# Routing tokens by indirect transfers instead of matmuls, a softmax from two exps, and a clamp on another engine, in a two-layer graph and state-space kernel

## The chip, the cores and the metric

The kernel runs on one core of a Trainium2 chip. The metric is the device time of one execution in microseconds; lower is better. Engines are named as the profile names them: PE is TensorE, DVE is VectorE, ACT is ScalarE, POOL is GpSimd, and SP is SyncE, which here only issues transfers. Each engine works through its own instructions in a fixed order, and an instruction that has to wait holds up all that stand behind it on that engine.

## What is computed

The input x holds 64 batches of 256 tokens with 256 features. Two layers follow each other; each is a graph attention part and then a feed-forward part, both added to x. `adj` is a random 256x256 adjacency matrix.

```python
# layer 0
x = x + gnn0(layernorm(x))    # MLP to 512, attention over all tokens, MLP to 256, attention masked by adj
x = x + ffn0(layernorm(x))    # only the top tokens go through the MLP
# layer 1
x = x + gnn1(layernorm(x))    # attention masked by adj
x = x + ffn1(layernorm(x))    # a Mamba-2 block: convolution, decays, chunk of 256

# each attention:
e = leaky_relu(f1[:, :, None] + f2[:, None, :], 0.2)   # f1, f2: one number per token
att = softmax(where(mask, e, -inf), axis=2)
out = elu(att @ h)

# ffn0:
weights = x @ wr + br                       # one number per token
sel_idx = top_k(weights, 128)[1][:, :127]   # the 127 best of 256 tokens
y = (gelu(x[sel_idx] @ w1 + b1) @ w2 + b2) * weights[sel_idx]
out = zeros.at[sel_idx].set(y) + x
```

In the Mamba block a matrix E of decays is needed for every head: the exp of the difference of two running sums, clamped so that the part that a triangular mask drops later does not overflow.

## The kernel before

A step works on a group of two batches, 512 tokens, that is four chunks of 128 tokens on the 128 partitions. There are 32 groups; the first and the last are worked on as two single batches. Everything is float32. A matmul of float32 stands in the trace as two passes, a transpose as one.

Each part of a layer is a Python generator that issues a few instructions and then yields. A lane is a sequence of such parts over the groups: lane a is `gnn0`, lane b is `ffn0` and then `gnn1`, lane c is `ffn1`; lanes d, e and f are the single batches at the two ends, and w prepares the weights. Strings written out by hand, `FIRST`, `ORDER` and `LAST` (lines 21 to 37), say which lane takes the next step: `FIRST` at the start, then `ORDER` again and again (one pass for one group), then `LAST`. So three groups are in work at a time, in different parts of the layers, and each engine's order is fixed when the program is built.

The places that the change touches, with the line numbers of the profile:

- `scores` (L422 to L474), the attention weights, three times per group. PE transposes the column f2 into a row `fb` (L430). DVE finds the largest (L437, or L446 with the mask), computes `top` for each of the four chunks (L439 or L450) and from it `nm`, minus the row's maximum (L455). ACT applies Prelu (the leaky relu, L459) and then Exp with the row's sum as a by-product (L463). DVE takes the reciprocal (L468) and POOL scales (L473). `turned` (L489) transposes the result on PE.
- `ffn0` (L597 to L705). After the layernorm, DVE computes each token's weight `wc` (L602, L605); PE spreads it as a row `wrow` (L610). DVE counts for each token how many have a larger weight, which is its rank (L622, L625), and compares the rank with 0 to 126 (`ranks`, L120 to L125) to form the 0-1 matrix `pick` (L628). PE multiplies by `pick` to gather the 127 tokens, already transposed (`psel`, L635), transposes `pick` (L645, copied as `pT`, L647), runs the MLP (`ph`, `py`), and multiplies by `pT` to send the results back to their tokens (`po`, L695). DVE combines (L702), POOL adds to x (L705).
- In `ffn1`, the row of running sums goes to DRAM (`csd`, L786 and L787) and comes back spread over all partitions as E, one 384 KB load per head (L809). `decays` (L814 to L826) clamps the two diagonal blocks of E with one DVE instruction (L820) and takes the exp on ACT (L826). Later DVE multiplies E by `cb` (L899) and PE uses it (`py`, L916).
- All matmuls are issued by a helper at L251 and all transposes by one at L254, so PE's rows are told apart by their tiles.

Of the kernel before, what the change touches and what calls it, by code (L numbers as in the profile page):

```python
# [9 lines left out]
I32 = mybir.dt.int32  # L10
BF16 = mybir.dt.bfloat16
# [10 lines left out]
    "dwddadadwaaadawdaaddadaddaaaaadddaaddaaaaddaddaddadaaadaddaddwawdaaaaaaadddadddawdaaaaadadaadaddbaba"  # L22
    "aaabaaaabbaawaaaabwaabaaaaababbbaabbbwababababbbbabaaaabaabaawabababbaaaaabbbaaabbbbabbbaababbababab"
    "baababbbaaaabbabbbabbbaaacwccaababcaababbaabcaaabaaabacabbabbbbbaaabaabaabcbcabaabwbbaacabbaabawabca"
    "bbbab"
)
ORDER = (
    "cAaaccbbbbbbacabaccccbccaabacccabcbccabaacbccacabcaaaacacacbcccccbcacabcccbcaaacacbbccccccacaaccbcac"
    "cbacacabccabcccbcbBabccaccbcccabbcacaacbaccacbcbaacbcbbcbcababcbbcbCccbbbbaacaacabcaabbcbbabbbbbccc"
)  # L30
LAST = (
    "ececefefceecbbceccbbcbffbbbccfcbbfceccebbfcccbefccbcbeceebfcccecccecccceccfbccbcecccbccbeeccbefceccf"
    "ccccccfeeebbccecccfecffffcccfbffebcccbfbceffbccbcccefebbcefcccfceeebcbccccbfefccbcccbfbffcbbccccbcbb"
    "cfceefcbfbbcfefcbbcffbfecccbfcbfefbbbfbfbccffeeeebffbeccccfffebbfebbefbecfcbccccccbcbbcbffcccbeeceec"
    "ebfecbbbbcebffcceccbccccbeccebccececbbefcccffecfccffccfecfebcebceeceecebcffbcfeccfffcfecfeccefcececc"
    "cfe"
# [4 lines left out]
def kernel(ctx: ExitStack, tc: tile.TileContext, a: dict, out: bass.AP):  # L41
# [78 lines left out]
    ranks = cons("ranks", P, P)  # L120
    with tc.tile_pool(name="first", bufs=1) as first:
        iota_i = first.tile([P, P], I32, tag="iota_i", name="iota_i")
        nc.gpsimd.iota(iota_i, pattern=[[1, P]], base=0, channel_multiplier=0)
        nc.vector.tensor_copy(ranks, iota_i)
    nc.vector.memset(ranks[:, KK:P], -1.0)  # L125
# [75 lines left out]
    for t, ap in ((dtb, a["L1_ffn_dt_bias"]), (negA, a["L1_ffn_A_log"])):  # L201
# [28 lines left out]
        "xn": 2, "pk": 3, "v": 2, "g": 4,  # L230
# [6 lines left out]
    def tiled(pool, shape, tag, name, bufs):  # L237
        return pool.tile(list(shape), F32, tag=tag, name=name, bufs=bufs)
# [4 lines left out]
    def sm(tag, *shape, bufs=4):  # L243
        return tiled(small, shape, tag, tag, bufs)

    def sized_sm(tag, n, most, *rest, bufs=4):

        return sm(tag, P, most, *rest, bufs=bufs)[:, :n]
# [39 lines left out]
    def made_ready():  # L288
# [19 lines left out]
        nc.vector.tensor_scalar(mask1, adj, 0.0, -1e37, ALU.is_le, ALU.mult)  # L308
# [31 lines left out]
        yield  # L340
        for t in (b1h, conv_w, conv_b, W_in[:, :, :DI]):
            nc.vector.tensor_scalar(t, t, 0.5, None, ALU.mult)
# [23 lines left out]
    def sized(G, own=None):  # L366
# [12 lines left out]
        def columns(tag, name, most=512):  # L379
            t = wide(lambda tag, name: t512(tag, name) if most == 512 else tiled(t2, (P, most), tag, name, 4), tag, name)  # L380
            return t[:, (own or 0) * N : (own or 0) * N + T]
# [40 lines left out]
        def scores(f1, f2, mask, strict, tag):  # L422
# [3 lines left out]

            yield
            fb = psum("fb")
            for c in range(C):
                tr(fb[:, tok(c)], f2(c).to_broadcast([P, P]), ident)  # L430
            halves = [slice(h * N, (h + 1) * N) for h in range(2)]
            es = [t512(tag, "e") for b in range(G)]
            rows = [fb[:, b * N : (b + 1) * N] for b in range(G)]
            top = sized_sm("top", C, 4)
            if mask is None:
                most = sized_sm("most", G, 2)
                nc.vector.tensor_reduce(most, fb[:, :T].rearrange("p (b j) -> p b j", b=G), AX.X, ALU.max)  # L437
                for c in range(C):
                    nc.vector.tensor_scalar(  # L439
                        top[:, c : c + 1], most[:, c // 2 : c // 2 + 1], f1(c), -1.0, ALU.add, ALU.mult  # L440
                    )
            else:
                most = sized_sm("topm", C, 4)
                for c in range(C):
                    e = es[c // 2][:, halves[c % 2]]
                    nc.vector.tensor_tensor_reduce(  # L446
                        e, rows[c // 2], mask[:, c % 2, :], 1.0, -3e38, ALU.add, ALU.max, most[:, c : c + 1]
                    )
                for c in range(C):
                    nc.vector.tensor_scalar(  # L450
                        top[:, c : c + 1], most[:, c : c + 1], f1(c), -1.0, ALU.add, ALU.mult
                    )
            yield
            nm = sized_sm("nm", C, 4)
            nc.vector.scalar_tensor_tensor(nm, top, ALPHA, top, ALU.mult, ALU.min)  # L455
            den = sized_sm("den", C, 4)
            for c in range(C):
                e = es[c // 2][:, halves[c % 2]]
                nc.scalar.activation(e, rows[c // 2] if mask is None else e, AF.Prelu, bias=f1(c), alpha=ALPHA)  # L459
            yield  # L460
            for c in range(C):
                e = es[c // 2][:, halves[c % 2]]
                nc.scalar.activation(e, e, AF.Exp, bias=nm[:, c : c + 1], accum_out=den[:, c : c + 1])  # L463
            yield
            if strict:

                nc.vector.scalar_tensor_tensor(den, nm, 1e30, den, ALU.is_lt, ALU.mult)
            nc.vector.reciprocal(den, den)  # L468
            if strict:
                nc.vector.scalar_tensor_tensor(den, nm, 1e30, den, ALU.is_lt, ALU.mult)  # L470
# [33 lines left out]
        def project(xT, w, tag):  # L504

            res = []
            for c in range(C):
# [4 lines left out]
                h = tiled(t2, (P, D + 2), tag, "hp", 4)  # L512
                nc.scalar.copy(h, pp[:, : D + 2])
# [3 lines left out]
        def aggregate(at, h, i):  # L517

            u = psum("u")
            for half in range(2):  # L520
                for j in range(2):
# [3 lines left out]
                        h[2 * i + j][:, :D],  # L525
# [4 lines left out]
        def gnn0(xt, of, early):  # L530
            xn = yield from layernorm(xt, *of, "o")
            xT = yield from transposed(xn, lambda: columns("h", "xT", H1 + 2))
# [9 lines left out]
            h1 = []  # L542
# [539 lines left out]
```

## Time and profile before

| what | us |
|---|---|
| median of 3 runs (lowest, highest) | 3656.5 (3651.49, 3656.68) |
| the profiled execution's own time | 3653.81 |
| its span | 3652.1 |
| PE busy | 3533.4 |
| DVE busy | 2842.1 |
| ACT busy | 2189.1 |
| POOL busy | 1146.8 |
| TensorE clock granted | 0.99 |
| DMA: 150.89 MB, mean 41 GB/s; the SP queue's packets took 12.1% of the 16 engines' span | |

Busy time is the time in which an engine executed something; waits are not in it. An engine's rows add up to less or more than its share where instructions overlap, as matmuls do. A row of the groups gives the line, the engine, what is written and read, the shape and the count, then the busy time and the mean of one in ns, then the idle time of the engine just before these instructions and what ended it. The chain that ended last is followed back from the last instruction; 81% of it lies on PE.

### The profile page before, as it was taken

Reading aid. Unit: us, or ns where it says so; the run is one execution under the profiler, and the core shown is the slowest. Engines: PE = TensorE matmul, PEld = TensorE weight load, DVE = VectorE, ACT = ScalarE, POOL = GpSimd, SP = SyncE. Lnnn points to the kernel's source line nnn. Section 1 sums busy time; section 2 is a strip of 40 time slices with the busy share of each in tenths; the row PEclk is TensorE's granted clock in tenths of the full one; section 3 lists DMA queues with packets and bytes.
Section 4 is the critical chain, followed back from the end, with each engine's and each line's share of the span. In section 5 each row is a group of like instructions: output and inputs, shape, how many; then the busy total and the mean of one; then the engine's idle time right before and its main releaser. Section 6 shows DMA issues by size and latency. Waiting matters only on the chain.

```text
span 3652.1 us, 50662 instructions
## 1 busy us (share of the span) xinstructions
PE 3533.4 (97%) x17004; PEld 2550.6 (70%) x17004; DVE 2842.1 (78%) x7275; ACT 2189.1 (60%) x4942; POOL 1146.8 (31%) x1274
## 2 busy tenths in 40 slices
PE   8999999999999999999999999999999999999876
PEld 6766776776776776776776776776776777776544
DVE  5577778777778777878777878777878777878776
ACT  4565665665665665666665666655666655666544
POOL 2223333323333323333323333323333323333222
PEclk9999999999999999999999999999999999999989
DMA  3011101111101111101111101111101111101111
GB/s 116 1 39 43 49 15 43 48 42 46 49 15 43 48 40 48 49 15 43 48 40 49 48 16 43 49 40 49 44 20 43 48 40 49 41 23 37 43 43 48
DMA packets 90260, 150.89 MB, mean 41 GB/s; under 512 B 12304, under 2 KB 57232, under 8 KB 90000
## 3 DMA queue, kind: packets, MB, share of 16 engines
q1 hardware_dynamic: 90000, 147.65, 12.1%
q8 instruction: 135, 2.21, 0.2%
q14 instruction: 125, 1.02, 0.1%
HBM read 125.86 MB, written 17.56 MB: 39 GB/s over the span
## 4 chain that ended last, share of the span: by engine, by line
PE 81%; DVE 12%; ACT 4%; issue 1%; POOL 1%; DMA 1%; SPq 0%; ACTq 0%; POOLq 0%; DVEq 0%
PE pp L251 31%; PE u L251 10%; PE py L251 9%; PE po L251 7%; PE pz L251 6%; PE pt L254 5%; PE ph L251 4%; PE pa L251 3%; PE psel L251 2%; DVE st L393 1%; DVE xt L595 1%; DVE g L674 1%; DVE w L498 1%; DVE g L671 1%; DVE w L594 1%; PE pss L251 1%
## 5 line engine op out<-in xcount | busy, mean ns | idle before, releaser
L251 PE MATMUL pp<-W_fc,o 128*128 128x256 f32 (+1 forms) x2048 | 460.1, 379 | 0.4 <-DVE W_fc L286 0.4
L845 DVE SCALAR_TENSOR_TENSOR xs<-pp,conv_w,xs 128x510 f32<-128x510 f32 (+5 forms) x495 | 359.9, 728 | 93.9 <-ACT xs L841 79.9
L251 PEld LDWEIGHTS pp<-W_fc,o 128*128 128x128 f32 x2048 | 381.9, 189 | 67.8 <-issue 15.9
L826 ACT ACTIVATE E<-E,ncs 128x256 f32<-128x256 f32 (+1 forms) x1024 | 382.0, 449 | 61.0 <-DVE E L820 58.3
L473 POOL TENSOR_SCALAR e<-e,den 128x256 f32<-128x256 f32 x384 | 186.8, 505 | 714.2 <-PE pp L251 350.3
L251 PE MATMUL pp<-xT,W_in 128*128 128x512 f32 (+1 forms) x660 | 303.6, 593 | 0.0
L850 ACT ACTIVATE th<-xs 128x512 f32<-128x512 f32 (+1 forms) x165 | 101.7, 617 | 326.6 <-DVE xs L845 311.4
L925 POOL TENSOR_TENSOR xs<-xs,gz 128x512 f32<-128x512 f32 (+1 forms) x132 | 205.9, 1561 | 203.0 <-DVE xs L924 200.5
L251 PE MATMUL py<-w,g 128*128 128x256 f32 x1024 | 236.2, 383 | 20.7 <-DVE g L674 20.7
L899 DVE TENSOR_TENSOR E<-E,cb 128x768 f32<-128x768 f32 (+1 forms) x264 | 250.5, 964 | 1.1
L705 POOL TENSOR_TENSOR xt<-xn,xt 128x512 f32<-128x512 f32 x64 | 81.3, 1270 | 526.1 <-DVE xn L702 525.9
L251 PE MATMUL pz<-xT,W_in 128*128 128x512 f32 (+1 forms) x528 | 242.8, 583 | 0.0
L567 POOL TENSOR_TENSOR o<-w,o 128x512 f32<-128x512 f32 (+1 forms) x132 | 180.7, 1369 | 197.8 <-DVE w L501 197.8
L251 PE MATMUL ph<-sel,w 128*128 128x256 f32 x1024 | 242.0, 379 | 0.0
L251 PE MATMUL po<-W_ol,xs 128*128 128x256 f32 x1024 | 241.3, 379 | 0.0
L251 PEld LDWEIGHTS py<-w,g 128*128 128x128 f32 x1024 | 190.0, 190 | 70.9 <-DVE g L674 46.7
L251 PE MATMUL pp<-xT,mlp_w 128*128 128x512 f32 (+1 forms) x528 | 236.5, 583 | 0.7 <-ACT xT L419 0.7
L251 PE MATMUL u<-at,h 128*128 128x256 f32 x1024 | 236.8, 379 | 0.0
L251 PE MATMUL pp<-o,mlp_w 128*128 128x512 f32 (+1 forms) x528 | 231.1, 590 | 2.9 <-POOL o L567 2.9
L820 DVE TENSOR_TENSOR E<-E,ccs 128x512 f32<-128x512 f32 (+1 forms) x264 | 224.3, 863 | 0.0
L393 DVE BATCH_NORM_STATS2 st<-xt 128x6 f32<-128x256 f32 x512 | 185.1, 413 | 49.7 <-POOL xt L750 23.4
L251 PEld LDWEIGHTS u<-at,h 128*128 128x128 f32 x1024 | 191.7, 190 | 37.6 <-issue 7.3
(179 smaller groups left out, 7722.3 us busy)
## 6 DMA issues: line engine op xcount, KB each, us to landing
E<-csd SPq DMA_DIRECT2D x248, 384.0 KB
xt<-in_x_dram SPq DMA_DIRECT2D x31, 512.0 KB
out_dram<-xt SPq DMA_DIRECT2D x31, 512.0 KB
cs<-xs SPq DMA_DIRECT2D x64, 64.0 KB
E<-csd SPq DMA_DIRECT2D x16, 192.0 KB
w<-in_L_ffn_w_dram SPq DMA_DIRECT2D x2, 1024.0 KB
W_in<-in_L_ffn_W_in_dram SPq DMA_DIRECT2D x1, 1160.0 KB
mlp_w<-in_L_gnn_mlp_w_dram SPq DMA_DIRECT2D x2, 512.0 KB
```

Of the source, the lines that this page charges most:

```text
L251: nc.tensor.matmul(to, lhsT, rhs, start=start, stop=stop)
L254: nc.tensor.transpose(to, of, eye)
L393: nc.vector.bn_stats(st[:, c, :], xt[:, c, :])
L473: nc.gpsimd.tensor_scalar(e, e, den[:, c : c + 1], 1.0, ALU.mult, ALU.mult)
L567: nc.gpsimd.tensor_tensor(o1[m], w, o1[m], ALU.add)
L705: nc.gpsimd.tensor_tensor(pair(xt, b), xn[b], pair(xt, b), ALU.add)
L820: nc.vector.tensor_tensor(diag, diag, ccs[:, :, :, h : h + 1].to_broadcast([P, G, 2, P]), ALU.min)
L826: nc.scalar.activation(e[:, b, to], e[:, b, to], AF.Exp, bias=ncs[:, b, half, h : h + 1])
L845: nc.vector.scalar_tensor_tensor(s3[:, :, d:], p3[:, :, : N - d], conv_w[:, m, 3 - d : 4 - d], s3[:, :, d:], ALU.mult, ALU.add)
L850: nc.scalar.activation(th, s, AF.Tanh)
L899: nc.vector.tensor_tensor(e2, e2, cb2, ALU.mult)
L925: nc.gpsimd.tensor_tensor(yt, yt, gz, ALU.mult)
```

## The change

Four things are changed, and the three strings that fix the order are written anew for them.

1. **Indirect transfers.** A new lane g (`ranked_tokens`) runs ahead of lane b. It computes the ranks as before, but the row of weights goes to DRAM and comes back spread over the partitions (`wrow` is now in SBUF). POOL issues four indirect transfers per group that write each token's normalised features to the row of its rank in a DRAM tile; the first 128 rows are read back (`taken`), and four transposes on PE make `psel` of them. After the MLP the results go to DRAM (`ranked`), and four more indirect transfers read for every token the row of its rank, or of rank 127 at most, where `valid` and the changed b2 put zeros. `pick`, `pT`, and the two multiplications by them are gone.
2. **Softmax.** Instead of Prelu and then Exp, ACT takes two Exps of the row, with scale 1 and with scale 0.2, and DVE takes the larger of the two and sums it. The columns f1 and f2 are copied to a tile of their own.
3. **Clamp of E.** Four POOL instructions of 128x128 per head take the place of one DVE instruction of 128x512.
4. **Buffers.** `xn` has four buffers in place of two, a tag `row` is added, small tiles have three buffers in place of four.

```diff
@@ scores
-            nm = sized_sm("nm", C, 4)
-            nc.vector.scalar_tensor_tensor(nm, top, ALPHA, top, ALU.mult, ALU.min)
...
-                nc.scalar.activation(e, rows[c // 2] if mask is None else e, AF.Prelu, bias=f1(c), alpha=ALPHA)
...
-                nc.scalar.activation(e, e, AF.Exp, bias=nm[:, c : c + 1], accum_out=den[:, c : c + 1])
+            nc.vector.scalar_tensor_tensor(m, top, ALPHA, top, ALU.mult, ALU.max)
+            nc.vector.tensor_tensor(b1, f[:, :, 0], m, ALU.subtract)
+            nc.vector.scalar_tensor_tensor(b2, f[:, :, 0], ALPHA, m, ALU.mult, ALU.subtract)
...
+                nc.scalar.activation(upper[c // 2][:, halves[c % 2]], rows[c], AF.Exp, bias=b1[:, c : c + 1])
...
+                nc.scalar.activation(e, rows[c], AF.Exp, bias=b2[:, c : c + 1], scale=ALPHA)
+                nc.vector.scalar_tensor_tensor(
+                    e, upper[c // 2][:, halves[c % 2]], 1.0, e, ALU.mult, ALU.max, accum_out=den[:, c : c + 1]
+                )
@@ project, and the same in gnn0
-                nc.scalar.copy(h, pp[:, : D + 2])
+                nc.scalar.copy(f[:, c, :], pp[:, D : D + 2])
+                nc.scalar.copy(h, pp[:, :D])
@@ ffn0, now ranked_tokens and ffn0
-            wrow = psum("wrow")
-            for c in range(C):
-                tr(wrow[:, tok(c)], wc[:, c : c + 1].to_broadcast([P, P]), ident)
+            row = rowd.tile([4 * P], F32, tag="row", name="row")[:T]
+            nc.sync.dma_start(row.rearrange("(c p) -> p c", p=P), wc)
+            yield
+            wrow = t512("row", "wrow")[:, :T]
+            nc.sync.dma_start(wrow, row.partition_broadcast(P))
...
-                nc.vector.tensor_scalar(pick[:, c, :], ranks, rank[:, c : c + 1], None, ALU.is_equal)
+            nc.vector.tensor_copy(to, rank)
+            nc.vector.tensor_scalar(back, rank, float(KK), None, ALU.min)
+            yield
+            sorted_x = [rowd.tile([N, D], F32, tag=f"sorted{b}", name="sorted") for b in range(G)]
+            for c in range(C):
+                nc.gpsimd.indirect_dma_start(
+                    sorted_x[c // 2], bass.IndirectOffsetOnAxis(ap=to[:, c : c + 1], axis=0), chunk(xn, c), None
+                )
+            yield
+            taken_x = t512("row", "taken")[:, : G * D]
+            for b in range(G):
+                nc.sync.dma_start(taken_x[:, b * D : (b + 1) * D], sorted_x[b][:P, :])
...
-                    for h in range(2):
-                        mm(
-                            psel[:, (k * G + b) * P : (k * G + b + 1) * P],
-                            chunk(xn, 2 * b + h)[:, k * P : (k + 1) * P], pick[:, 2 * b + h, :],
-                            start=(h == 0), stop=(h == 1),
-                        )
+                    tr(
+                        psel[:, (k * G + b) * P : (k * G + b + 1) * P],
+                        taken_x[:, b * D + k * P : b * D + (k + 1) * P], ident,
+                    )
...
-                nc.vector.tensor_tensor(y[:, b * D : (b + 1) * D], py[:, b * D : (b + 1) * D], b2, ALU.add)
+                nc.vector.scalar_tensor_tensor(
+                    y[:, b * D : (b + 1) * D], py[:, b * D : (b + 1) * D], valid, b2, ALU.mult, ALU.add
+                )
+            ranked_y = [rowd.tile([P, D], F32, tag=f"ranked{b}", name="ranked") for b in range(G)]
             for b in range(G):
-                yield
-                po = psum("po")
-                for h in range(2):
-                    mm(
-                        po[:, h * D : (h + 1) * D], pT[:, tok(2 * b + h)], y[:, b * D : (b + 1) * D],
-                        start=True, stop=True,
-                    )
+                nc.sync.dma_start(ranked_y[b], y[:, b * D : (b + 1) * D])
+            yield
+            ws = [t512("g", "w") for b in range(G)]
+            for c in range(C):
+                nc.gpsimd.indirect_dma_start(
+                    chunk(ws, c), None, ranked_y[c // 2], bass.IndirectOffsetOnAxis(ap=back[:, c : c + 1], axis=0)
+                )
@@ decays
-                diag = e.rearrange("p b (k l) -> p b k l", k=3)[:, :, ::2, :]
-                nc.vector.tensor_tensor(
-                    diag, diag, ccs[:, :, :, h : h + 1].to_broadcast([P, G, 2, P]), ALU.min
-                )
+                for b in range(G):
+                    for half, to in enumerate((slice(0, P), slice(N, N + P))):
+                        nc.gpsimd.tensor_scalar(
+                            e[:, b, to], e[:, b, to], ccs[:, b, half, h : h + 1], 1.0, ALU.min, ALU.mult
+                        )
```

In the built program PE has 512 instructions fewer (9984 to 9472), DVE 35 fewer, ACT 224 more, POOL 1281 more and SP 192 more.

## Prediction, made before the changed kernel was run

> **What bounds the kernel now.** I read the page's busy shares first, then the busy time of one period, then the chain that ended last, then the rows of the operations that the diff touches. All figures are of one profiled execution (span 3652.1 us, its own time 3653.8 us); the median of the runs is 3656.5 us, 2.7 us above it. I predict from 3653.8 and leave that difference in the range.
>
> ```profile
> span 3652.1 us, 50662 instructions
> ...
> PE 3533.4 (97%) x17004; PEld 2550.6 (70%) x17004; DVE 2842.1 (78%) x7275; ACT 2189.1 (60%) x4942; POOL 1146.8 (31%) x1274
> ...
> 1526.97:1636.71 109.74, 108.79 (x530) 78.65 (x529) 87.67 (x223) 67.81 (x153) 35.85 (x40) 1.00 0.12 40
> ...
> 1507.43 0.44 PE wrow L254 x4
> ...
> 1514.65 1.78 PE psel L251 x16
> 1516.43 0.44 PE pt L254 x4
> ...
> 1549.20 0.86 PE po L251 x4
> ...
> 1556.93 0.86 PE po L251 x4
> ```
>
> The window is one steady period (one group of two batches, from one store of the output to the same store a group later): of 109.74 us TensorE is busy 108.79, VectorE 87.67, at a granted clock of 1.00. Only 0.95 us per group is TensorE idle, so a period is TensorE's work, and every microsecond taken off its queue shortens the period until another engine or a wait takes over. The chain lines give the true price of a group of matmuls, since there they follow each other without overlap: 128x128 transposes 0.11 us each, the 16 passes that pick tokens 1.78, the four passes of each `po` 0.86.
>
> **TensorE: what goes.** Per group the change deletes the spread of the weights (`wrow`, 0.44), the transposes of `pick` (0.44), both `po` groups (1.72), and puts four transposes (0.44, as the `pt` row) in place of the 1.78 of `psel`. That is 0.44 + 0.44 + 1.72 + 1.34 = 3.94 us; 32 groups give 126 us. Nothing is added on TensorE: `fb` has four transposes as before. This lies on the path: 3653.8 - 126 = 3527.8 if nothing else becomes late.
>
> **VectorE, ScalarE, GpSimd: the balance.**
>
> ```profile
> L820 DVE TENSOR_TENSOR E<-E,ccs 128x512 f32<-128x512 f32 (+1 forms) x264 | 224.3, 863 | 0.0
> ...
> L628 DVE TENSOR_SCALAR pick<-ranks,rank 128x128 f32<-128x128 f32 x128 | 38.0, 297 | 4.6
> ...
> L602 DVE SCALAR_TENSOR_TENSOR junk<-xn,wr 128x256 f32<-128x256 f32 x128 | 54.0, 422 | 3.3
> ...
> L463 ACT ACTIVATION_READ_ACCUMULATOR e<-e,nm 128x1 f32 x384 | 79.5, 207 | 0.0
> ...
> L473 POOL TENSOR_SCALAR e<-e,den x384: 476/482/1825, 30.1 to 3549.7; 128x256 f32<-128x256 f32 x192
> ...
> L669 POOL TENSOR_SCALAR g<-g x128: 620/626/835, 102.1 to 3515.3; 128x512 f32<-128x512 f32 x128
> ...
> L266 POOL TENSOR_SCALAR r<-r x33: 193/194/196, 307.9 to 3642.3; 128x4 f32<-128x4 f32 x31, 128x2 f32<-128x2 f32 x2
> ...
> 1539.86 0.29 SPq L787 DMA_DIRECT2D csd<-csT  x1
> ...
> 1541.14 3.21 SPq L809 DMA_DIRECT2D E<-csd  x6
> ```
>
> (In the three POOL lines the figures after the count are the shortest, median and longest ns.) VectorE loses the clamp of E (224.3), `pick` (38.0), three of four small `top` operations in each of three scores (384 x 0.206 = 79 less 98 x 0.16 = 16) and `nm` (98 x 0.157 = 15): 340 in all. It gains the maximum with its sum, 384 x (422 + 80 for the accumulator read, as L602 has it) = 193, three small ones per scores (98 x 3 x 0.157 = 46) and two conversions per group (64 x 0.18 = 12): 251. Net -89: 2842 becomes 2753, 78% of 3528, as before. Reading `wrow` and the gathered rows from SBUF instead of PSUM, and `valid` in L690's place, I cost at nothing: at most 320 x 0.06 us = 19 either way (L622's 479 against L602's 422), inside VectorE's slack of 20%; without that slack it is 19 us.
>
> ScalarE: Prelu becomes an Exp of the same size (475 to 526 ns against 516), so nothing; the accumulator reads (79.5) and the copy of `pT` (18.9) go, and 256 two-column copies of f come at about 0.20 us (an activation of one column took 197 ns) = 51. Net -47, 61% of the new span. The loads of activation tables stay at 67.
>
> GpSimd: 1024 clamps of 128x128. No row has that size; the 4-column row (0.19) and the 256-column row (0.48) bound one; the line through the rows of 256 and 512 columns gives 0.40, the one through 4 and 256 gives 0.33; I take 0.37, 379 us. With 256 indirect transfers at 1.0 us (below) GpSimd has 1147 + 379 + 256 = 1782 us, 51%. A head's clamp goes from 0.86 us on VectorE to 4 x 0.37 = 1.5 us on GpSimd; ScalarE's exp waits for it, and behind that exp stand the PSUM copies that TensorE needs. In the new order the clamps of a steady head stand about 3 us of TensorE work ahead of their exp, which covers 1.5; without that cover it is 8 x 0.6 = 5 us a group.
>
> [...] L473's median of 482 is 6 ns over its shortest and its mean is 505, beside a VectorE that is 80% busy, so 6% was lost. I take some 30 us on VectorE, hidden.
>
> **The added waits.** The order of the changed kernel's instructions, priced on TensorE with the durations above, shows the windows that the plan leaves.
> First, the scatter. The four scatters go to two DRAM tiles; the second into each waits for the first to land, and GpSimd stands still meanwhile. Behind it are the fourth's turn, then the four scalings of e (L473's), for which TensorE's transposes wait; SP waits for each pair to read it back, and `psel` waits for that. With L from issue to landing and g of GpSimd per transfer: first scatter to e's transposes, 7.4 us of TensorE work, needs 2L + 2g + 0.5; first scatter to `psel`, 10.4 us, needs 3L + g + R, R being the read back.
> No row of before has an indirect transfer. Near is SP's: the 4 KB write issued at 1539.86 had landed when the read of it was issued at 1541.14, 1.28 us; 128 KB adds some 0.7 (512 KB of output in the 2.88 us after its issue). So R = 2.0, and L is at least 1.3. [...] I take L = 2.3; the row alone would give 2.0. For g the ends are SP's 0.29 us an issue and 2.4 (the longest GpSimd row, L756); I take 1.0. Then the two needs are 7.1 and 9.9 against 7.4 and 10.4: covered, with 0.3 and 0.5 us to spare. By the row it is covered with more. As it is so thin I charge 0.3 us a group, 10 us.
> Second, the way back. From the writes of y to the first combination on VectorE stand about 5 us, to the third 10; needed are R + L = 4.3 and R + 3g + L = 7.3. Covered; else VectorE stands with the convolution behind it, whose PSUM banks TensorE waits for.
> Third, row and `wrow`: 14 us of TensorE work between issue and first use, against two landings (2.8): covered. SP's queue is passed by the reads of `taken`, the writes of y and the row; the six loads of E are issued about 10 us ahead of the writes of y, which they would otherwise hold up. In the last two groups the order leaves under 1 us between gather and reader: 2 x 2.5 = 5 us.
>
> **Sum:** 3653.8 - 126 + 10 + 5 = 3543 us.
>
> **Rivals.**
> (a) The chain of serialised scatters decides, and the kernel is slower. Gain and loss meet at 3.94 us of wait per group: 3L + g = 12.3 or L + g = 5.4, for instance L = 3.6 and g = 1.6. With L = 3.8 and g = 2.2 the e transposes are 5.1 late and `psel` 5.2: +166 - 126, 3694 us. For it: nothing in the profile prices the transfers, and the order has no more than half a microsecond to spare. [...]
> (b) A part is given back: GpSimd's clamps and transfer issues run late and ScalarE waits, or contention costs VectorE more, 1 to 2.5 us a group (32 to 80 us): about 3590. For it: ScalarE and VectorE stand in step with TensorE within half a microsecond. Against: 20% slack on VectorE, 49% on GpSimd.
> (c) The queue's own waits shrink too, as VectorE has less ahead of the transposes: at most the 0.95 us idle per group, 30 us: 3505.
> (d) The saving isn't there because TensorE's passes were hidden. The chain has them on it and the period is 99% TensorE: under 3%.
>
> **How the numbers follow.** The forecast (3520 to 3580) has 0.50, (b) 0.22, (c) 0.04, gain and loss meeting within 0.2% (7 us, about what a measurement can tell) 0.05, (a) beyond it 0.19. So faster 0.76, same 0.05, slower 0.19. The range is 3505 to 3670: it takes in (c), (b) and the start of (a), since L and g are not known. The range of faster cases alone is 3505 to 3620.
>
> **What would show it.** Right: a period of 105.5 to 106.5 us with TensorE idle about 1 us; `psel` with four transposes of 0.11; indirect transfers that hold GpSimd about 1 us and land within 2.5; E's exp not waiting for GpSimd. Wrong: waits of TensorE on e's scaling (GpSimd) or on the read of `taken`, of VectorE's combination on the gather, of ScalarE's E on GpSimd, with a total over 100 us; or g over 1.5 us.

## The result, and the profile after

The changed kernel takes 4061.2 us (median of 4 runs, 4059.91 to 4064.45) against 3655.5 us before (now the median of 4 runs): ratio 1.1113, 95% interval 1.1094 to 1.1133. It is slower by 406 us where 3543 us was forecast, and outside the range. The profiled execution took 4060.97 us of its own, with a span of 4059.3.

From the page of the changed kernel: the span, the busy shares, the chain that ended last by engine, and three groups.

```profile
span 4059.3 us, 51076 instructions
...
PE 3599.3 (89%) x16108; PEld 2520.3 (62%) x16108; DVE 2876.4 (71%) x7624; ACT 2193.0 (54%) x4782; POOL 2240.1 (55%) x2555
...
POOL 29%; DVE 22%; PE 21%; issue 14%; ACT 8%; DMA 7%; SPq 0%; POOLq 0%; DVEq 0%; ACTq 0%
...
L846 POOL TENSOR_SCALAR E<-E,ccs 128x128 f32<-128x128 f32 x1024 | 859.8, 854 | 19.3 <-DMA E<-csd 13.9
L852 ACT ACTIVATE E<-E,ncs 128x256 f32<-128x256 f32 (+1 forms) x1024 | 426.5, 449 | 293.2 <-POOL E L846 292.9
...
L925 DVE TENSOR_TENSOR E<-E,cb 128x768 f32<-128x768 f32 (+1 forms) x264 | 336.4, 1306 | 1.0
```

The last of these rows is VectorE's product of E with `cb`, called E*cb below. In the kernel before, the rows of the exp and of this product read:

```profile
L826 ACT ACTIVATE E<-E,ncs 128x256 f32<-128x256 f32 (+1 forms) x1024 | 382.0, 449 | 61.0 <-DVE E L820 58.3
...
L899 DVE TENSOR_TENSOR E<-E,cb 128x768 f32<-128x768 f32 (+1 forms) x264 | 250.5, 964 | 1.1
```

No engine is full any more. The chain, 81% on PE before, is spread over four engines. The clamp on GpSimd takes 0.85 us on average where 0.37 was taken, and ScalarE's exp stands 293 us for it, where it stood 58 us for VectorE's clamp before.

Now the windows of the changed kernel: three pieces around one gap of TensorE, and a stretch of one mean period. After the bounds and the length stand the busy times of PE, PEld, DVE, ACT and POOL, then the granted clock.

```profile
2043.90:2046.31 2.41, 0.21 (x1) 0.00 (x0) 2.41 (x6) 0.00 (x0) 1.29 (x2) 1.00 0.31 94
2046.31:2047.40 1.09, 0.83 (x6) 0.59 (x7) 0.31 (x1) 0.00 (x0) 1.09 (x4) 1.00 0.33 120
2047.40:2050.81 3.41, 3.41 (x18) 1.72 (x16) 0.03 (x1) 1.75 (x3) 2.79 (x3) 0.53 0.58 189
...
2060.00:2181.46 121.46, 110.00 (x488) 76.02 (x489) 87.71 (x232) 66.45 (x146) 69.88 (x79) 0.96 0.17 51
```

The period (last row) is 121.5 us in place of 109.7, with TensorE idle for 11.5 us of it. In the first row TensorE stands for 2.4 us (the last matmul before it ends 0.2 us into the row); about a microsecond after it comes back its clock goes to half for 3.41 us (third row, 0.53 as the row starts 0.21 us ahead of the stretch). In stretches at half clock a pass of 128x256 of `u` or `py` starts 427 ns after the one before it, at full clock 216 (medians), so 3.41 us of matmuls cost 1.7 us on top of the gap's length. The trace has 11 stretches at half clock before the change, all in the head and the tail, and 78 after it.

This gives an account that I use for the kernels below, worked out from the trace over 26 whole groups: gaps (no matmul runs for over 0.25 us), clock (half of the matmul time at half clock), and the rest.

| us a group | period | gaps | clock | rest |
|---|---|---|---|---|
| before | 109.73 | 0.56 | 0.00 | 109.17 |
| after | 121.45 | 10.32 | 3.55 | 107.58 |

26 periods are 305 us of the loss; the head (to the 2nd group's norm) is 41 us longer and the tail (from the 28th's) 62. The gaps of a group in the changed kernel stand before `u` (3.06 us, for ScalarE's copy `ag`), before `pt` of e (2.6, GpSimd's scaling), before the last `py` of the MLP (2.0, VectorE's g), and 2.6 in smaller ones. One of each:

```profile
2073.18 1.99 PE L252 MATMUL py<-w,g 128*128 128x256 f32 x8 [2.03 <-DVE g L695]
...
2131.85 1.47 PE L252 MATMUL u<-W_l,ag 128*128 128x256 f32 x5 [3.06 <-ACT ag L758]
...
2169.06 0.93 PE L255 MATMUL pt<-ident,e 128*128 128x128 f32 x4 [2.41 <-POOL e L480]
```

The largest one, before `u`, comes from the clamp. GpSimd works on the eight clamps of two heads for 7.6 us, ScalarE's exps follow it one by one, and `ag` stands behind them:

```profile
2122.20 7.60 POOL L846 TENSOR_SCALAR E<-E,ccs 128x128 f32<-128x128 f32 x8
...
2129.83 0.40 ACT L852 ACTIVATE E<-E,ncs 128x128 f32<-128x128 f32 x1 [0.18 <-POOL E L846]
...
2131.23 0.57 ACT L758 COPY ag<-pa 128x512 f32<-128x512 f32 x1
```

The gap before `pt` is the predicted scatter chain: GpSimd's timeline ahead of it, then VectorE's reciprocal for the scaling and TensorE's last work before the gap.

```profile
2159.53 1.01 POOL L268 TENSOR_TENSOR r<-r,neghalf 128x4 f32<-128x4 f32 x1
2160.72 1.13 POOL L648 DMA_INDIRECT sorted<-xn,to  x1 [0.18 <-issue]
2163.55 0.98 POOL L648 DMA_INDIRECT sorted<-xn,to  x1 [1.70 <-DMA sorted<-xn,to]
2164.84 0.96 POOL L648 DMA_INDIRECT sorted<-xn,to  x1 [0.30 <-issue]
2167.52 0.96 POOL L648 DMA_INDIRECT sorted<-xn,to  x1 [1.72 <-DMA sorted<-xn,to]
2168.52 1.88 POOL L480 TENSOR_SCALAR e<-e,den 128x256 f32<-128x256 f32 x4
...
2166.16 0.18 DVE L475 RECIPROCAL den<-den 128x4 f32<-128x4 f32 x1
...
2159.58 7.07 PE L252 MATMUL po<-W_ol,xs 128*128 128x256 f32 x32
```

Twice GpSimd stands 1.7 us for a landing. VectorE had the reciprocal for the scaling at 2166.34, so the four scatters made it 2.2 us late, nearly the whole gap.

The rows by line in the changed kernel (shortest, median, longest ns) that answer to those of before:

```profile
L846 POOL TENSOR_SCALAR E<-E,ccs x1024: 704/712/2206, 254.3 to 4036.1; 128x128 f32<-128x128 f32 x171
...
L480 POOL TENSOR_SCALAR e<-e,den x384: 471/481/952, 31.0 to 3953.8; 128x256 f32<-128x256 f32 x192
...
L690 POOL TENSOR_SCALAR g<-g x128: 621/626/1140, 122.2 to 3904.8; 128x512 f32<-128x512 f32 x128
...
L648 POOL DMA_INDIRECT sorted<-xn,to x128: 957/980/1247, 98.8 to 3858.9; - x128
```

The transfers cost GpSimd the 1.0 us that was taken. The multiplications are where they were. Only the clamp, the one with `min`, is off: 0.71 us in the median.

### The profile page after: what moved, and what is told of

The parts are those of the page before. It is cut to its first block, busy times and chain, and to the rows that moved or that the text cites. A ratio compares the mean times of both kernels' runs of the same rounds, so it can differ in the third digit from the quotient of the medians.

```text
span 4059.3 us, 51076 instructions
## 1 busy us (share of the span) xinstructions
PE 3599.3 (89%) x16108; PEld 2520.3 (62%) x16108; DVE 2876.4 (71%) x7624; ACT 2193.0 (54%) x4782; POOL 2240.1 (55%) x2555
## 4 chain that ended last, share of the span: by engine, by line
POOL 29%; DVE 22%; PE 21%; issue 14%; ACT 8%; DMA 7%; SPq 0%; POOLq 0%; DVEq 0%; ACTq 0%
POOL E L846 14%; PE pp L252 8%; PE py L252 4%; PE pt L255 3%; DVE E L925 3%; DVE st L396 3%; DMA w<-ranked,back 3%; POOL rstd L268 2%; DVE xs L871 2%; POOL sorted L648 2%; DMA sorted<-xn,to 2%; POOL o L577 2%; POOL e L480 2%; POOL g L690 2%; POOL xs L951 1%
## 5 line engine op out<-in xcount | busy, mean ns | idle before, releaser
L846 POOL TENSOR_SCALAR E<-E,ccs 128x128 f32<-128x128 f32 x1024 | 859.8, 854 | 19.3 <-DMA E<-csd 13.9
L852 ACT ACTIVATE E<-E,ncs 128x256 f32<-128x256 f32 (+1 forms) x1024 | 426.5, 449 | 293.2 <-POOL E L846 292.9
L690 POOL TENSOR_SCALAR g<-g 128x512 f32<-128x512 f32 x128 | 105.9, 827 | 517.7 <-ACT g L689 517.7
L252 PE MATMUL py<-w,g 128*128 128x256 f32 x1024 | 274.9, 423 | 70.7 <-DVE g L695 70.6
L925 DVE TENSOR_TENSOR E<-E,cb 128x768 f32<-128x768 f32 (+1 forms) x264 | 336.4, 1306 | 1.0
L252 PE MATMUL py<-E,xd 128*64 128x256 f32 (+1 forms) x2048 | 224.8, 340 | 54.6 <-DVE E L925 46.1
L252 PE MATMUL u<-at,h 128*128 128x256 f32 x1024 | 259.6, 400 | 2.0 <-ACT at L496 2.0
L505 DVE TENSOR_SCALAR w<-w 128x512 f32<-128x512 f32 (+1 forms) x196 | 97.4, 497 | 227.4 <-ACT w L503 227.4
L252 PEld LDWEIGHTS py<-E,xd 128*64 128x64 f32 x2048 | 142.9, 140 | 175.0 <-issue 65.9
L508 DVE SCALAR_TENSOR_TENSOR w<-w,u 128x512 f32<-128x512 f32 (+1 forms) x196 | 132.0, 674 | 164.3 <-ACT w L506 164.2
```

The costliest lines, as they stand in the source:

```text
L252: nc.tensor.matmul(to, lhsT, rhs, start=start, stop=stop)
L508: nc.vector.scalar_tensor_tensor(w, w, -1.0, u, ALU.add, ALU.max)
L690: nc.gpsimd.tensor_scalar(g, g, 8 * GELU_A * GELU_C, 2 * GELU_C, ALU.mult, ALU.add)
L846: nc.gpsimd.tensor_scalar(e[:, b, to], e[:, b, to], ccs[:, b, half, h : h + 1], 1.0, ALU.min, ALU.mult)
L852: nc.scalar.activation(e[:, b, to], e[:, b, to], AF.Exp, bias=ncs[:, b, half, h : h + 1])
L925: nc.vector.tensor_tensor(e2, e2, cb2, ALU.mult)
```

## The experiments

Times are medians; the kernel before ran on the same chip each time (3653 to 3655 us).

### The clamp

**e1**: the changed kernel with the clamp back on VectorE, one `min` of 128x512.

> The changed kernel with the clamp of E back on VectorE as one 128x512 instruction per head; everything else, the order too, is the changed kernel's. Theory A (the clamp on GpSimd, 0.85 us an instruction where 0.37 was predicted, makes everything late): 3530 to 3620 us, and ScalarE's wait for GpSimd on E (293 us) gone. Rival B (the serialised scatters and the gather make it late): above 3900 us, with TensorE's waits on the scaling of e unchanged (217 us).

4016.4 us, ratio 1.0995 (1.0963 to 1.1027). My first theory, that the clamp alone is the loss, falls; the time is rival B's, and TensorE's waits on the scaling of e stay (215 us). In the new order a clamp on VectorE isn't cheap either: ScalarE's exp waits 193 us for it. The gap before `u` is gone, but new ones of 1.6 us stand before `fb` and of 1.45 before the MLP's `pp`.

**e2**: the kernel before with only the GpSimd clamp.

> The kernel before with the four GpSimd clamps per head as the only edit. Theory A: the clamp alone costs most of the 406 us, 3850 to 4200 us, with 1024 instructions of about 0.85 us on GpSimd. Rival B: within 1% of 3655 us, since GpSimd is idle for two thirds of the span.

3914.4 us, 1.0716 (1.0685 to 1.0747): theory A held. 261 us, from one moved operation; TensorE's gaps before the `py` that reads E are 4.7 us a group, where the kernel before has none.

**e3**: the changed kernel with `ALU.add` for `ALU.min`.

> The changed kernel with min replaced by add in the GpSimd instruction (no clamp is computed: the column is added instead). Theory A1 (min is a slow operation on GpSimd): the add takes 0.33 to 0.40 us and the time is 3540 to 3640 us. Theory A2 (any instruction of that shape is slow there, or is slowed by VectorE): about 0.8 us and about 4060 us. Rival B: about 4060 us whatever the instruction takes.

3868.8 us, 1.0591 (1.056 to 1.0622). Its row by line:

```profile
L846 POOL TENSOR_SCALAR E<-E,ccs x1024: 361/367/1937, 253.8 to 3847.5; 128x128 f32<-128x128 f32 x171
```

An addition of the same shape takes 0.367 us, what the prediction took for the clamp. So its estimate was right for the operations that it came from, and `min` costs double (0.712 us in the median). That is 192 of the 406 us, and the gap before `u` falls from 3.06 to 0.66. A1 was right on the price and wrong on the time: the rest is elsewhere.

**e4**: forms of the clamp: `min` alone for odd heads, and 256 columns at once for even ones.

> The changed kernel with two other forms of the clamp: on odd heads min alone without the multiplication by 1, on even heads the first block 256 columns wide in place of 128 (the result is the same). If the second operation costs, odd heads take about 0.4 us an instruction; if the price is per element of min, they stay at 0.7 and the 256-column ones take about 1.2 us; if it is a fixed cost, these take about 0.85.

4070.3 us (one run). GpSimd's groups by form:

```profile
L849 POOL TENSOR_SCALAR E<-E,ccs 128x256 f32<-128x256 f32 x256 | 375.4, 1467 | 18.9 <-DVE xs L874 18.1
L847 POOL TENSOR_SCALAR E<-E,ccs 128x128 f32<-128x128 f32 x512 | 323.5, 645 | 0.6
L849 POOL TENSOR_SCALAR E<-E,ccs 128x128 f32<-128x128 f32 x256 | 203.2, 794 | 0.0
```

These means include clamps that were held up by VectorE. In the median 128 columns took 0.71 us, 256 took 1.16, as the per-element case had it, and `min` without the multiplication took 0.595 for 128. So most of the price goes with the elements of `min`, and about 0.1 us with the multiplication by 1. Neither form as tried here made the kernel faster; `min` alone for all heads was not tried.

### The transfers

**e5**: e3 with the scatters to the two DRAM tiles in turn.

```diff
-            for c in range(C):
+            for c in ((0, 2, 1, 3) if C == 4 else (0, 1)):
                 nc.gpsimd.indirect_dma_start(
```

> The kernel of e3 (the clamp of E is left out, a column is added in its place), with one change: the four scatters are issued in the order 0, 2, 1, 3, so that the second goes to the other DRAM tile and only the third waits, for a landing that is already under way. In e3 TensorE stands 2.4 us per group before the transposes of e, since the scaling of e stands on GpSimd behind four scatters of which two wait 1.7 us each for a landing. Theory A (serialised scatters are a part of the loss): the scatters take 5 us in place of 7.8, the gap shrinks to under 1 us, the time falls by 45 to 100 us, to 3770 to 3825. Rival B (TensorE waits there for something else, the sums of the softmax): the gap stays over 2 us and the time stays within 15 us of 3869.

3800.7 us, 1.0394 (1.0373 to 1.0414): 68 us less, and the gap before `pt` is 0.33 us. Theory A held.

**e7**: e3 with the tokens moved by matmuls again.

> The kernel of e3 (the clamp of E left out, a column added in its place) in the new order and with the new softmax, but with the tokens picked and sent back by matmuls as in the kernel before; no indirect transfer is left. TensorE has 3.94 us a group more (126 us). Theory A (of the 216 us that e3 is above the kernel before, only the serialised scatters ahead of e's scaling belong to the transfers, about 2.4 us a group and the slower clock after it): 3860 to 3930. Rival B (the transfers cost far more than the matmuls that they replace, over 6 us a group): below 3800.

3867.7 us, 1.0586 (1.0568 to 1.0603), the time of e3, within theory A's range: with the scatters in this order the transfers pay for themselves and no more.

### The softmax and the order

**e6**: the kernel before with the new softmax alone; **e16**: the same without the maximum.

> The kernel before, with its own order, with only the new softmax (two exps, the maximum with its sum on VectorE, the two columns of f copied apart); tokens by matmuls and the clamp on VectorE as before. Theory A (the softmax as such costs nothing): VectorE has 80 us more or less, TensorE stays at 99% of a period, time 3630 to 3700. Rival B (the softmax is a part of the loss, since its maximum is a further step between ScalarE and the sum): over 3720, with TensorE waiting before the transposes of e.

> The softmax alone in the order of the kernel before (3799 us, period 114.1 us) with the maximum left out: both exps are computed, the second is used, with its row sum as a by-product on ScalarE. Theory A (the maximum on VectorE is the price of the softmax): period 109.7 to 110.5 us, time 3650 to 3680. Rival B (the copies of f or the two exps on ScalarE are): over 3740.

e6: 3799.0 us, 1.0393 (1.0375 to 1.041), rival B's time. e16: 3716.8, 1.0168 (1.0151 to 1.0185). The softmax that I costed as a gain costs 145 us in the old order: 82 are the maximum, 62 the two exps with the copies of f and the small steps around them. Neither theory of e16 is met in full.

**e9**: the changed kernel's softmax and transfers in the old order, clamp on VectorE.

> The changed kernel with the order of the kernel before: the clamp back on VectorE, the new softmax, the transfers (scatters in the order 0, 2, 1, 3); the steps of lane g are set into the old order about 70 us ahead of the MLP, and the way back at the places of the old multiplications. The counterpart is the old order with the new softmax alone (3799 us, period 114.1 us). Theory A (the transfers do save TensorE 3.9 us a group where nothing stands behind them): period 109.5 to 112, time 3680 to 3760. Rival B (the transfers bring waits of their own wherever they stand): period 114 or more, 3800 or more.

4086.8 us, 1.1191 (1.1172 to 1.121), with new gaps of 2.4 us before `fb` and 1.8 before the `py` that reads E. It shows that where I put the steps is bad, and nothing of the transfers: inconclusive.

**e11**: the kernel before with the clamp as relu on ScalarE.

```diff
-                nc.vector.tensor_tensor(diag, diag, ccs..., ALU.min)
+                nc.scalar.activation(diag[:, b, half, :], diag[:, b, half, :], AF.Relu, bias=ccs..., scale=-1.0)
...
+                nc.scalar.activation(diag, diag, AF.Exp, scale=-1.0)
```

> The kernel before, with the clamp of E taken off VectorE in another way: ScalarE takes relu(ccs - E) of the four diagonal blocks (four instructions) and the exp of minus that in one instruction for all four blocks, with two more for the blocks beside them; no engine is waited for in between. VectorE loses 224 us, ScalarE gains about 8 x 0.5 us a group. Theory A (what made the clamp on GpSimd slow is its price and its place ahead of ScalarE, so a clamp that stays on ScalarE costs nothing, and TensorE's 0.95 us of idle time a group is all that is to be had): 3620 to 3665. Rival B (ScalarE becomes late and the copies out of PSUM with it): over 3680.

3736.6 us, 1.0229 (1.0212 to 1.0246). VectorE is 158 us less busy (2684.5), and the kernel is slower, as rival B had it: ScalarE is 212 us busier (2401.5; the relu of 128x128 took 0.39 us), and a gap of 1.3 us a group appears before the `py` that reads E. ScalarE's share of 60% said nothing of this place.

### Repairs

**e8**: the changed kernel with a masked addition for the clamp, the scatters earlier and in turn, and the residual's step behind the last g; **e12**: relu on ScalarE, scatters in turn, the same step; **e10**: e5 with this step moved, nothing else.

> The changed kernel, with the whole computation, and three repairs: in place of four clamps one GpSimd instruction per head adds -2**120 to the part of E that the triangle drops (tensor_tensor 128x512, priced from the 1.27 us of the 128x512 products of GpSimd), the scatters in the order 0, 2, 1, 3 and moved ahead of the scaling of the previous output, and the last part of gnn0's residual behind the last g on VectorE. Theory A (the loss is made of waits: the price of min on GpSimd, scatters ahead of e's scaling, VectorE's residual ahead of g, and the slower clock that each gap brings): the gaps of 2.4 and 2.0 us are gone, granted clock 0.98 or more, time 3540 to 3640. Rival B (the new order can't keep TensorE busy whatever is repaired): over 3700.

> The changed kernel with the whole computation and three repairs: the clamp as relu on ScalarE (as in the run beside this one), the scatters in the order 0, 2, 1, 3, and the residual's step behind the last g. Theory A (the loss consists of these waits and of the slower clock that follows each): period 108 to 111 us, time 3620 to 3730. Rival B (new order and softmax keep a loss of their own): over 3760.

> The kernel with interleaved scatters (3801 us; clamp left out, a column added in its place), with one step of the order moved: the last part of gnn0's residual with the layernorm's sums, 3 us of VectorE, stands behind the last two g operations in place of ahead of them. Theory A (the 2.04 us for which TensorE stands before the last py of every group is VectorE's queue): the gap falls to under 0.7 us and the time by 35 to 70 us, to 3730 to 3765. Rival B (the gap is the length of the chain from ph to g, or shows up at the next reader): within 15 us of 3801.

e8: 4157.6 us, 1.1376 (1.1357 to 1.1395). GpSimd, waiting for the ranks, held up the gate's product behind the scatters, and TensorE stood 5.5 us before `pss`. e12: 3878.3, 1.0617 (1.0599 to 1.0635). Both are rival B's. e10: 3850.5, 1.0544 (1.0527 to 1.0562), slower than e5 by 50, which neither theory had. VectorE's timeline of e10 behind the last g:

```profile
1738.03 0.69 DVE L695 SCALAR_TENSOR_TENSOR g<-g,v 128x512 f32<-128x512 f32 x1 [0.70 <-ACT g L693]
...
1739.96 1.40 DVE L396 BATCH_NORM_STATS2 st<-xt 128x6 f32<-128x256 f32 x4
...
1741.55 2.28 DVE L871 SCALAR_TENSOR_TENSOR xs<-pp,conv_w,xs 128x510 f32<-128x510 f32 x3
...
1747.48 0.73 DVE L408 TENSOR_SCALAR xn<-xt,mv,rstd 128x256 f32<-128x256 f32 x2
```

The gap before `py` went from 2.04 to 0.69 us, and one of 2.65 appeared before the transposes of `xn`. For the 10 us from g to `xn` VectorE has no idle time: the wait is that of a full stretch and moves to the next reader. No repair of mine beats the kernel before.

### What is left

These kernels leave out parts of the computation, to price them. **e14**: e5 with no clamp; **e15**: without the maximum too; **e17**: e15 with matmuls for the transfers.

> The kernel with interleaved scatters (3801 us, period 113.25 us) with no clamp of E on any engine: the GpSimd instructions are left out, and the exp takes E plus the column instead of E minus it, so that nothing overflows. Theory A (GpSimd's work on E costs VectorE by contention): E*cb falls from 1306 to about 965 ns, that is 2.7 us a group, and the period by 1.5 to 4 us, time 3670 to 3755. Rival B (the contention is hidden): E*cb faster, but the time within 30 us of 3801.

> As the run without a clamp, and the maximum of the two exps is left out as well: the second exp is taken as it is, its row sum a by-product on ScalarE, the first exp is computed and not used. VectorE loses 12 x 0.5 us a group. Theory A (VectorE and the hop over it are what is left of the loss): period 105.5 to 108 us, time 3490 to 3600, the saving that was forecast. Rival B (the transfers or the order hold TensorE whatever VectorE does): 3650 or more.

> As e15 (no clamp, no maximum, new order), but with the tokens picked and sent back by matmuls as in the kernel before: TensorE has 3.94 us a group more, VectorE 0.3 us of pick per chunk more. Theory A (where VectorE and GpSimd have room, the transfers save what was forecast, 126 us): 90 to 140 us above e15. Rival B (the transfers save nothing in this order, since their waits eat it): within 50 us of e15.

e14: 3762.6 us, 1.0295 (1.0277 to 1.0312). e15: 3757.9, 1.0282 (1.0264 to 1.0299). e17: 3821.5, 1.0459 (1.0441 to 1.0476). e14 is 38 us below e5, between the ranges of its two theories. Here the maximum costs 5 us, so e15's theory A falls. The transfers save 64 us of the 126 (e17 against e15), between the ranges again. And E*cb did not fall in e14: its mean is still 1304 ns. So the clamp isn't what slows it. The trace of e15 shows what does; first GpSimd, then VectorE:

```profile
1520.39 1.39 POOL L945 TENSOR_TENSOR xs<-xs,gz 128x512 f32<-128x512 f32 x1 [0.23 <-DVE xs L944]
1522.20 1.38 POOL L576 TENSOR_TENSOR o<-w,o 128x512 f32<-128x512 f32 x1 [0.42 <-DVE w L507]
```

```profile
1522.37 2.89 DVE L919 TENSOR_TENSOR E<-E,cb 128x768 f32<-128x768 f32 x2
```

The first of these two products starts 0.17 us after a GpSimd addition of two tensors and takes 2.02 us, 1.21 of them until the addition ends; the second takes 0.95. In e15, as in the changed kernel, 90 of the 248 products of 128x768 take over 1.5 us, about three of the eight of a group; in the kernel before 2 do, and 28 take 1.24.

**e18**: e14 with these GpSimd operations on one tensor; **e19**: the residual's step moved as well.

> The kernel without a clamp and with interleaved scatters (3763 us, period 112.15 us), with two of GpSimd's products of two tensors left out: the output of each head pair is not multiplied by its gate, and gnn0's residual is not added; a GpSimd instruction on one tensor of the same size stands in their place (0.62 us for 1.27). Theory A (the meetings of GpSimd's and VectorE's two-tensor instructions are a part of the loss): the three slow E*cb of a group fall from 2.02 to 0.95 us, VectorE by 100 us, and the time by 30 to 90 us, to 3670 to 3730. Rival B (they lie in VectorE's slack): E*cb faster, the time within 15 us of 3763.

> As the run without these products, with the last part of gnn0's residual behind the last two g operations on VectorE (the step that only moved the wait in the kernel with the clamp). Theory A (VectorE's queue is what TensorE waits for there, and with the products gone it can catch up): the gap of 2.04 us a group is under 0.7, no new gap of over 1 us takes its place, and the time is 30 to 70 us below the run without the products. Rival B (the stretch is full on VectorE with or without the products, and the wait moves to the transposes of gnn0's input): within 20 us of that run or above it.

e18: 3753.9 us, 1.0278 (1.0261 to 1.0295), period 112.14 against 112.15: E*cb's mean fell to 1069 ns (the slow ones to 1.36 us) and the time moved by 9 us, within rival B's 15, so contention there lies in slack and theory A falls. e19: 3796.1, 1.0388 (1.0371 to 1.0405), the wait moved to `xn` again (2.65 us), as rival B had it.

The account of the groups in the kernels that carry the argument:

| us a group | period | gaps | clock | rest |
|---|---|---|---|---|
| e3, add for min | 115.37 | 6.16 | 2.19 | 107.02 |
| e5, scatters in turn | 113.25 | 4.06 | 0.59 | 108.60 |
| e14, no clamp | 112.15 | 3.28 | 0.98 | 107.89 |
| e15, no maximum | 111.95 | 3.18 | 0.92 | 107.85 |
| e17, matmuls | 114.73 | 3.21 | 0.39 | 111.13 |
| e6, old order, softmax | 114.12 | 2.59 | 0.00 | 111.53 |

## Why the prediction was wrong, step by step

Taken out one after another, the parts of the 406 us are: `min` on GpSimd in place of an addition 192 (e3), the order of the scatters 68 (e5), what was left of the clamp 38 (e14), the maximum 5 (e15). The other 103 stay in e15, although the transfers save 64 there. Another sequence would share them out differently, since the waits cover each other: in the old order the maximum alone is 82.

- **TensorE: what goes.** Right in size: between e17 and e15 the rest falls by 3.28 us a group, between e7 and e3 by 4.69, where 3.94 was forecast. But it is what TensorE's queue loses, not what the period loses, and the step was used as the gain itself.
- **GpSimd: the clamp at 0.37 us.** This step failed, and it is the largest part: 0.71 us in the median, 0.85 on average, and GpSimd 2240 us where 1782 was the sum. The rows behind the estimate were all multiplications and additions, and for an addition it holds to 3 ns (e3). Its cover of "about 3 us" is less than a head's four clamps (4 x 0.85 = 3.4), and two heads follow each other (7.6 us in the timeline). Price: 192 us for `min` against an addition in the new order; 261 for moving the clamp at all in the old one.
- **The scatter.** The mechanism was right, its sizes were not. The first need, put at 7.1 us, is 8.3 in the timeline: 7.8 to the end of the fourth scatter and 0.5 for the first scaling. L = 2.3 was an assumption that no row of before showed (the one near it gave 2.0). It was close: a scatter landed after 2.4 us in the median, 3.2 at most; but the next one into the same tile starts 2.7 to 2.8 us after the first (58 of 64 times). The window, put at 7.4 us, is 5.9: the first scatter starts at 2160.72, about 1 us after the ranks were ready, behind GpSimd's norm (the first line of its timeline), and TensorE's work ends at 2166.65. 8.3 less 5.9 is the gap. The read back took 3.6 to 3.8 us on the chain (e3 and the changed kernel) where R was 2.0, but TensorE stood only 9.7 us in all for it. The charge was 10 us; 68 were to be had by the order of the scatters alone. g was right.
- **VectorE: slack of 20%.** VectorE's sum was forecast at 2753 us and is 2876, most of the difference in E*cb (+86). The sum does not decide (e18), and neither does the maximum in the new order (e15). What holds TensorE up in e10 is a stretch where VectorE is full while its share of the span is 74%. In the old order the same maximum costs 82 us.
- **Contention.** The 30 us for VectorE were my estimate and too small: E*cb takes up to 2.03 us for 0.95, 86 us in all, and each of the 90 that take over 1.5 us in the changed kernel starts within a GpSimd instruction on two tensors (61 in the product `xs`, 29 in the addition `o`). I looked at the added operations; these meetings are of old ones that the new order brings together. Where E*cb and the clamp meet, the clamp is held up (1.74 us for 0.71) and E*cb is not (0.95; last section).
- **The clock** was taken as 1.00. Of the 78 gaps of 2 us or more in the 26 groups of the changed kernel, 52 come with a stretch at half clock that begins between 1.0 us before their end and 1.6 us after it: 3.55 us a group. In e5 only 4 of 26 do, in e15 14 of 26, so such a gap doesn't always bring one.
- **The end of the program** was charged 5 us; head and tail together are 103 us longer. In e7, which has no transfers, they still are 49 us longer than before.
- **The rivals.** The slower case (a) named the scatters at 3694 us; they are a sixth of what happened. (b) named the late clamps and was given 1 to 2.5 us a group; `min` alone makes it 6.1 (e3). They were weighed as alternatives, and came together, each with its clock loss. (c) is a slip in the sum: 3543 less 30 is 3513, not 3505. Of the signs listed as "wrong" these are there: TensorE's waits on e's scaling (217 us), ScalarE's on the clamp (293), VectorE's on the gather (51, in 60 places).

Left open: with clamp and maximum out and the scatters in turn (e15) the period is 6.2 us above the 105.8 forecast. Gaps are 2.6 of it and the clock 0.9; with matmuls for the transfers they are there too (e17: 3.21 and 0.39), so they belong to the new order or to the two exps, which no run parts. The other 2.6 lie in the rest: in e15's trace the transposes of `xn` are 1.0 us a group longer than before, short waits included, `ph` 0.7 and `pz` 0.4, waits that the trace doesn't part from matmuls. In the old order the two exps with the copies of f add 1.0 to the rest (e16: 110.2 against 109.2). Not tried were the new order with the old softmax, the transfers in the old order without the new softmax, and the buffer counts apart from the order, since every kernel in the new order has them. Nothing here says whether an order that suits the transfers would be faster.

## What to carry to other kernels

A price is that of an operation, not of an engine and a shape: here `min` took 0.712 us on GpSimd where the addition of the same shape took 0.367 (e3), so where only another arithmetic operation has a row, keep the range open to double. In this kernel, where TensorE idled 0.95 us of 109.74, an engine's share of slack covered none of three longer steps (GpSimd in e2, 261 us; VectorE in e6, 145; ScalarE in e11, 84); ask of each longer step what stands behind it in that stretch. And count a TensorE gap of 2 us or more as its length and at times 1.7 us more (at 52 of 78 such gaps in the changed kernel, 14 of 26 in e15, 4 of 26 in e5).

## What the hardware showed that I had not expected

- GpSimd's `min` with a per-partition column and a multiplication: 0.712 us for 128x128 in the median, against 0.367 for the addition (e3); 1.16 us for 256 columns (e4).
- In the 26 groups of the changed kernel TensorE's clock halves 53 times, for 3.41 us (three times 6.83): 52 times at a gap of 2.03 to 4.06 us, from 1.0 us before its end to 1.6 us after it, and once after one of 1.37. 26 other gaps of 2.03 to 3.24 us had none. In the same groups of the kernel before, whose gaps are all under 0.6 us, it never halves.
- Who is held up depends on the pair. Between E*cb and a GpSimd product of two tensors it is mostly the one that starts second: E*cb takes 2.02 us for 0.95, the product 1.96 for 1.28 (`xs`, medians in the changed kernel; 1.44 where E*cb starts within it). Between E*cb and a clamp it is the clamp: 0.71 us apart from E*cb, 1.74 if it starts within one (29 of 31), 1.41 or 2.20 if it starts within the first of two and the second starts within it (29 and 29 of 60); the E*cb that starts second then takes 0.95.
- A chain of transfers over DRAM: 0.98 us of GpSimd for each scatter, 2.4 to its landing, 2.7 to 2.8 us to the next into the same tile, 3.62 (e3) and 3.76 us (the changed kernel) to read 128 KB back.
